# Four graph layers on one core: where layer 1's first four rows get their exponentials and logarithms, one scaling of layer 0's last rows, and which engine makes layer 1's bf16 casts

## The chip, the cores and the metric

The kernel runs on 1 core of one Trainium2 chip. The metric is the device time of one execution in microseconds (us), lower is better. The program is one launch; all four layers run in it one after the other.

## The reference, cut to what matters

The input is a field x of 8 batches, 2048 nodes and 64 features, and a symmetric 0/1 matrix adj of 2048 x 2048 with about eight neighbours a node. Four graph layers follow each other, each inside "add the input, then normalise over the 64 features". Layers 0 and 1 are the ones that matter here:

```
def _L0_gnn_ref(input, adj, W, a, ...):
    x = input * node_weights[None, :, None] + node_bias[None, :, None] + input
    h = layer_norm(x @ W) * ln_gamma + ln_beta
    e = leaky_relu(s1[:, :, None] + s2[:, None, :], 0.2)      # s1 = h.a1, s2 = h.a2
    att = softmax(where(adj > 0, e, -9e15), axis=-1)
    return elu(att @ h + h)

def _L1_gnn_ref(x, w0, b0, wa, ba, adj):
    feat = softplus(x * (INV_SQRT2 * w0[0, 0]) + b0[0])        # ln(1 + exp(.))
    scores = feat * wa + ba
    attn = softmax over the neighbours j of scores[j]           # per feature
    return sum_j attn * feat

x = _layernorm(x + _L0_gnn_ref(x, ...), axis=-1)
x = _layernorm(x + _L1_gnn_ref(x, ...), axis=-1)
...                                                             # layers 2 and 3
```

Since layer 1's score depends on the neighbour j alone, each node has one row of pairs (exp(score), exp(score) * feat), and layer 1 is a sum of these rows over the neighbours, followed by a division.

## The kernel before, in words

The 2048 nodes are 16 tiles of 128 (NT = 16; a tile is a partition dimension of 128 nodes, and 8 batches x 64 features = 512 values a node). X holds the field of all tiles and is updated in place.

Layer 0 first finds each node's neighbours from adj, and makes a table htab0 of h in memory. Then comes a pipeline of 17 steps, `step(0)` to `step(16)`. Step k handles tile k: GpSimd gathers its neighbours' rows (`fetch`, 10 indirect DMAs a tile, always one step ahead, three buffers hs), `weights` makes the attention weights (VectorE L598 and L601, ScalarE exponentials L602 and L603), `weigh` multiplies the gathered rows by them (VectorE L613, five a step) and TensorE adds them up (L621 values, L622 denominators). In the same step the tile before is finished: `divide(k-1)` (VectorE reciprocal L629, eight ScalarE scalings L632 of the sum po), `combine(k-1)` (VectorE L637, ScalarE exponential L639 into the tile e), `activate(k-1)` (VectorE L645, which reads e, and L648, which reads po for the last time), and `look_at(k-1)`, the statistics of the normalisation (L663). `solve` works out the inverse deviations for a group of tiles at a time (groups of 4, 4, 4, 2, 1 and 1), so a group of four is ready two steps after its last tile has been weighed. At the end of each step, `normalise` scales finished tiles on ScalarE (L183, eight instructions of 128x64 a tile); the last two tiles, 14 and 15, are scaled on VectorE after the steps (`normalise_here`, L683). Until the last tiles have been listed (step 12), the steps also carry the listing of neighbours of later tiles.

At the end of step 15 the kernel before makes feat for the first four tiles of layer 1: four exponentials (`exp_soon`, L699) and four logarithms (L764) into the tile `soon`, which lives through both layers.

Layer 1 makes its rows tile by tile. For tile t: `weight(t)` (VectorE L858: feat times wa; ScalarE L859: its exponential), `row(t)` (VectorE L863: the product with feat; SyncE L865: the row is written to the table rtab; and a cast of the row to bf16, on GpSimd L867 for odd t and on ScalarE L869 for even t), `second(t)` (VectorE L873: row minus its cast; ScalarE L874: that rest cast to bf16) and `third(t)` (VectorE L877: what is still left, as bf16). So a row is three bf16 pieces, and TensorE adds each piece into the sums of the first three output tiles (`add_piece`, L882, six matmuls of 512 columns a piece, 288 in all). feat for tiles 4 to 9 and 10 to 15 is made in two batches in between: exponentials one by one (`exp_of`, L847), and the logarithms of a batch together (`log_of`, L850). Then output tiles 3 to 7 are added from the pieces by dense products (`add_rows`, L817), mixed with tiles 8 to 15, whose neighbours' rows are gathered from rtab (`fetch` and `add_edges`, L946). The six sums of the first three output tiles take six of the eight PSUM banks; which banks these are is given by what layer 0 frees, and the last of layer 0 to be freed are those of tile 15: e after L645, po after L648.

The order of the work: steps 0 to 16 stand in one region in which the program's own order holds on TensorE, ScalarE, VectorE and GpSimd, and layer 1's row loop stands in a second such region. Within a region an engine's order is that of the program. The two regions are merged by the framework's scheduler: in the profile, instructions of the second region stand between those of the first on an engine (the eight L632 of tile 15, for instance, alternate with layer 1's L859, L847 and L869). [...] Layer 1's buffers lie in the memory that layer 0 has released: by the tile sizes in the code, the buffers of the row r lie over the gathered rows of tile 13, the first of them also over the end of tile 14's, and the pieces R of tiles 0 to 9 lie over what the listing used.

Of the kernel before, what the change touches and what calls it, by code (L numbers as in the profile page):

```python
# [48 lines left out]
def kernel(ctx: ExitStack, tc: tile.TileContext, ins: dict, out: bass.AP):  # L49
# [3 lines left out]
    NT = N // P  # L53
# [124 lines left out]
    def normed(chunks, stats):  # L178
        rstd, nmr = stats
        for c, v in enumerate(chunks):  # L180
            for b in range(B):
                k = c * B + b
                nc.scalar.activation(v[:, b], v[:, b], AF.Identity, scale=rstd[:, k:k + 1], bias=nmr[:, k:k + 1])  # L183
# [57 lines left out]
    SOON = 4  # L241
# [205 lines left out]
    def neighbours(it):  # L447
        on, plist, _, tops = lists[it]
        topf = tops.rearrange("p k m -> p (k m)")
        nbr = ap_.tile([P, SL + 1], F16, name="nbr")  # L450
        lists[it] = on, plist, nbr
        ops = []
        for k in range(0, SL, 8):
            ops.append(lambda k=k: nc.vector.max(nbr[:, k:k + 8], topf))
            if k + 8 < SL:
                ops.append(lambda k=k: nc.vector.match_replace(topf, nbr[:, k:k + 8], topf, 0.0))
        return ops

    def places(it):
        on, plist, nbr = lists[it]  # L460
        poff = plist[:, CW // 2 - 3:CW // 2]
        far_off = ap_.tile([P, 1], F32, name="far_off")
        nbrs = ap_.tile([P, NG, SL + 1], F16, name="nbrs")
        apart = ap_.tile([P, GE], F16, name="apart")
        lists[it] = on, plist, nbr, nbrs, apart

        def ended():
            nc.vector.scalar_tensor_tensor(ends[:, it:it + 1], offs[:, it:it + 1], -2.0, deg[:, it:it + 1], op0=ALU.mult, op1=ALU.subtract)
            nc.scalar.activation(apart, node_half, AF.Abs, scale=2.0, bias=ends[:, it:it + 1])

        return [lambda: nc.vector.tensor_reduce(far_off, poff, AX.X, ALU.max),
                lambda: nc.vector.tensor_scalar(offs[:, it:it + 1], far_off, 2.0 * GE, depth[:, 1:2], op0=ALU.min, op1=ALU.mult),
                ended,
                lambda: nc.vector.tensor_copy(nbr[:, SL:SL + 1], offs[:, it:it + 1]),
                lambda: nc.vector.tensor_tensor(nbrs, nbr.unsqueeze(1).to_broadcast(nbrs.shape),
                                                group.unsqueeze(2).to_broadcast(nbrs.shape), ALU.mult)]

    def tests(it):
        on, nbr = lists[it][0], lists[it][2]
        junk = ap_.tile([P, P], BF16, name="junk", bufs=1)  # L480
        return [lambda: nc.vector.scalar_tensor_tensor(junk, on[:, it * P:(it + 1) * P], 1.0, ident_bf, op0=ALU.mult, op1=ALU.mult,
                                                       accum_out=own_edge[:, it:it + 1]),
                lambda: nc.vector.scalar_tensor_tensor(junk[:, 0:SL], nbr[:, 0:SL], 0.0, nbr[:, 0:SL], op0=ALU.is_gt, op1=ALU.logical_and,
                                                       accum_out=listed[:, it:it + 1])]

    def select(it):
        _, plist, _, nbrs, apart = lists[it]
        nc.vector.tensor_scalar(SelT[:, it], apart, deg[:, it:it + 1], None, op0=ALU.is_lt, saturate=False)
        pl = plist[:, 1:1 + GS * NG * (SL + 1)].rearrange("p (g l) -> p g l", l=SL + 1)
        ps = plist[:, CW // 2:CW // 2 + GE].rearrange("p (s n) -> p s n", n=P)  # L490
        for s in range(GS):
            sel = SelT[:, it, s * P:(s + 1) * P]
            nc.tensor.matmul(pl[:, s * NG:(s + 1) * NG], sel, nbrs, start=True, stop=True)
            nc.tensor.matmul(ps[:, s], sel, ident_h, start=True, stop=True)
        lists[it] = pl, ps
# [63 lines left out]
    held, zs, stats = {}, {}, {}  # L559
# [117 lines left out]
    def normalise(it):  # L677
        normed([X[:, it]], stats.pop(it))

    def normalise_here(it):  # L680
        rstd, nmr = stats.pop(it)
        for b in range(B):
            nc.vector.tensor_scalar(X[:, it, b], X[:, it, b], rstd[:, b:b + 1], nmr[:, b:b + 1], op0=ALU.mult, op1=ALU.add)  # L683
# [5 lines left out]
    def interleaved(a, b):  # L689
# [5 lines left out]
                got.append(b.pop(0))  # L695
        return got

    def exp_soon(t):
        nc.scalar.activation(soon[:, t], X[:, t].rearrange("p b d -> p (b d)"), AF.Exp, scale=w0, bias=bb)  # L699

    def step(k):

        listed_, odd = AHEAD + k // 2, k % 2
        now, before_, ahead = k < NT, 1 <= k <= NT, k + 1 < NT
        early_, mid, late = [], [], []
        if odd and listed_ < NT:
            early_ = neighbours(listed_) + tests(listed_) + places(listed_)
            mid = [lambda: select(listed_)]
            if listed_ + 1 < NT:
                ats[listed_ + 1] = load(listed_ + 1)  # L710
        if not odd:
            if listed_ - 1 in lists:
                early_ = sources(listed_ - 1)
            if listed_ < NT:
                late = list_even(listed_)
        chain = []
        if k >= 2 and k - 2 < NT and k - 2 == norm_of[k - 2][-1]:
            chain = solve(norm_of[k - 2])
        if ahead:
            fetch(k + 1)  # L720
        main_a = weights(k) if now else []
        group = [weigh(k, n) for n in range(len(TOGETHER))] if now else [[]] * len(TOGETHER)
        if not odd and listed_ - 1 in lists:
            main_a.append(lambda: edges(listed_ - 1))
        main_a += group[0][:1]
        if before_:
            main_a.append(lambda: divide(k - 1))
        if ahead:
            main_a.append(lambda: prepare(k + 1))
        main_a += group[0][1:]  # L730
        main_b = group[1][:1]
        if before_:
            main_b.append(lambda: combine(k - 1))
        main_b += group[1][1:]
        main_b += activate(k - 1) if before_ else []
        main_c = list(group[2])
        main_c += look_at(k - 1) if before_ else []

        def run(main_, side, skip):
            done_, total = 0, len(side)  # L740
            for i, op in enumerate(main_):
                op()
                share = total * (i + 1 - skip) // max(1, len(main_) - skip)
                while done_ < share:
                    side[done_]()
                    done_ += 1
            for op in side[done_:]:
                op()

        half = (len(chain) + 1) // 2  # L750
        run(main_a, interleaved(early_[:len(early_) // 2], chain[:half]), 3)
        if ahead:
            scores(k + 1)
        if not odd and listed_ < NT:
            mark(listed_)
        run(main_b, interleaved(early_[len(early_) // 2:], chain[half:]), 0)
        for op in mid:
            op()
        run(main_c, late, 0)
        if k == NT - 1:  # L760
            for t in range(SOON):
                exp_soon(t)
            for t in range(SOON):
                nc.scalar.activation(soon[:, t], soon[:, t], AF.Ln, bias=ones_col)  # L764
        for t in sorted(stats)[:1 if k < NT - 3 else 2]:
            if t < NT - 2:
                normalise(t)

# [8 lines left out]
    with tc.manual_schedule(engines=engines):  # L777
        fetch(0)
        prepare(0)
        scores(0)  # L780
        for k in range(NT + 1):
            step(k)
        for op in solve(norm_of[NT - 2]) if norm_of[NT - 2] in sts else []:
            op()
        for op in solve(norm_of[NT - 1]):
            op()
        for t in sorted(stats):
            normalise_here(t)
    adj_.close()
    l0.close()  # L790

# [9 lines left out]
    with ExitStack() as l1:  # L801
# [50 lines left out]
        def split(v):  # L852
            return v.rearrange("p (h n) -> p h n", h=2)
# [7 lines left out]
        def row(t):  # L861
            r = rs_[t]
            nc.vector.tensor_tensor(r[:, :, 1], split(fs[t]), r[:, :, 0], ALU.mult)  # L863
            rf = r.rearrange("p h a n -> p (h a n)")
            nc.sync.dma_start(rtab[t * P:(t + 1) * P, :], rf)  # L865
            if t % 2:
                nc.gpsimd.tensor_copy(piece[t][0], rf)  # L867
            else:
                nc.scalar.copy(piece[t][0], rf)  # L869
# [460 lines left out]
    with early, ExitStack() as heads:  # L1330
# [261 lines left out]
        with tc.manual_schedule(engines=engines):  # L1592
# [37 lines left out]
            t = NT - 1  # L1630
# [17 lines left out]
    with ExitStack() as fifth:  # L1648
# [17 lines left out]
        hss, hsTs, pes, ws, wxs, zs, stats, sums = ({} for _ in range(8))  # L1666
# [257 lines left out]
    with tc.If(bad > 0), ExitStack() as anyway:  # L1924
# [88 lines left out]
        with ExitStack() as l0:  # L2013
# [71 lines left out]
            for b in range(B):  # L2085
                p, k = divmod(b, 2)
# [374 lines left out]
```

## Time and profile before

| | |
|---|---|
| Time, median of 3 runs | 1612.18 us (1601.11 to 1620.49) |
| The profiled execution's own time | 1768.37 us |
| Its span, first to last instruction | 1766.6 us |
| TensorE clock granted, mean over the span | 0.867 |
| TensorE busy | 1409.4 us (80%) |
| VectorE busy | 1165.4 us (66%) |
| ScalarE busy | 884.2 us (50%) |
| GpSimd busy | 790.0 us (45%) |

The profile is of one execution, and that one took 156 us longer than the median of the timed runs. Durations and waits are read from it as they stand; a difference that is worked out from it is a difference of the profiled execution. An engine's share of the span is an average over four layers with different limits; what counts for this change is the stretch from about 330 us (step 9 of layer 0) to about 670 us (the end of layer 1's products).

### The profile page before, as it was taken

The numbers are of one execution on the slowest core, as the hardware profiler recorded it, in microseconds if no ns is written. First come the engines' busy times: TensorE is split into PE (matmuls) and PEld (weight loads), VectorE is DVE, ScalarE is ACT, GpSimd is POOL, SyncE is SP. The second block draws the span as 40 slices with busy tenths as digits, with TensorE's granted clock in tenths as the row PEclk, the third lists the DMA queues.
The fourth block names the chain that finished last, engine by engine and source line by source line (L and its number), as shares of the span: only waits on it lengthen the run. The fifth ranks groups of instructions, "written<-read, shape, count | busy, mean of one in ns | idle before, by whom it ended". The sixth has DMA issues, their size and how long they took to land.

```text
span 1766.6 us, 39998 instructions
## 1 busy us (share of the span) xinstructions
PE 1409.4 (80%) x16140; PEld 956.7 (54%) x16140; DVE 1165.4 (66%) x2846; ACT 884.2 (50%) x1843; POOL 790.0 (45%) x786
## 2 busy tenths in 40 slices
PE   4775567755899996989728999998989679889884
PEld 4764233322343334522227777777777567777773
DVE  6787578776985646655834666666666536656667
ACT  4553245558833225445634565656555324555564
POOL 1234666661235552656433333343333156666651
PEclk9965575676899998999958999999999879888997
DMA  5434767662247971366434565656565365666651
GB/s 166 126 127 131 211 214 232 179 195 82 102 167 262 328 273 43 128 176 182 123 90 106 151 178 152 172 154 167 161 161 153 89 202 167 179 174 177 181 163 45
DMA packets 159322, 285.71 MB, mean 162 GB/s; under 512 B 68986, under 2 KB 94586, under 8 KB 157050
## 3 DMA queue, kind: packets, MB, share of 16 engines
q0 software_dynamic: 56320, 190.10, 36.5%
q1 hardware_dynamic: 86168, 88.78, 16.8%
q10 hardware_dynamic: 16640, 4.20, 1.0%
q8 instruction: 129, 2.11, 0.5%
q14 instruction: 65, 0.53, 0.1%
HBM read 242.52 MB, written 40.48 MB: 160 GB/s over the span
## 4 chain that ended last, share of the span: by engine, by line
PE 50%; DVE 9%; ACT 6%; issue 4%; DMA 1%; POOL 1%; another core or an unknown queue 1%; SPq 0%; POOLq 0%; ACTq 0%; DVEq 0%
PE pscore L1388 10%; PE po L1413 6%; PE pa L817 6%; PE ps L1716 4%; PE po L1755 4%; PE pt L1693 3%; PE pa L946 2%; PE pscore L1351 2%; PE pa L1290 2%; PE py L1120 2%; PE pscore L1480 2%; PE pe L1686 2%; PE pt L1000 2%; ACT w L1391 1%; DVE w_mid L1394 1%
## 5 line engine op out<-in xcount | busy, mean ns | idle before, releaser
L218 POOL DMA_INDIRECT xs<-xtab,src x160 | 171.8, 1074 | 280.8 <-PE po L1413 241.6
L218 POOL DMA_INDIRECT hs<-ktab,src x160 | 158.5, 991 | 140.2 <-DMA utab<-hT 47.7
L218 POOL DMA_INDIRECT hs<-htab,src x160 | 157.1, 982 | 88.5 <-issue 43.3
L1388 PE MATMUL pscore<-U,xsT 64*128 64x64 f32 (+2 forms) x2560 | 165.8, 280 | 1.1 <-ACT xsT L1375 1.1
L1388 PEld LDWEIGHTS pscore<-U,xsT 64*128 64x128 f32 x2560 | 155.2, 193 | 5.2 <-ACT xsT L1375 1.3
L1391 ACT ACTIVATE w<-pscore 128x512 f32<-128x512 f32 (+1 forms) x128 | 75.8, 622 | 139.7 <-PE pscore L1388 139.3
L1394 DVE SCALAR_TENSOR_TENSOR w<-w,Sel 128x512 f32<-128x512 f32 (+1 forms) x128 | 89.3, 722 | 79.2 <-ACT w L1391 61.1
L183 ACT ACTIVATE X<-X,ln_m,ln_r 128x64 f32<-128x64 f32 x240 | 81.4, 427 | 73.5 <-DVE ln_m L175 59.5
L1755 PE MATMUL po<-hs,w 128*32 128x65 f32 x2048 | 89.4, 236 | 32.3 <-issue 23.4
L1716 PE MATMUL ps<-U,hsT 128*128 128x64 f32 x768 | 104.5, 287 | 8.8 <-issue 5.8
L1716 PEld LDWEIGHTS ps<-U,hsT 128*128 128x128 f32 x768 | 103.0, 210 | 9.8 <-issue 6.0
L218 POOL DMA_INDIRECT rs<-rtab,src x80 | 75.9, 949 | 69.9 <-PE pa L946 47.5
L613 DVE TENSOR_TENSOR hs<-hs,w 128x1024 f32<-128x1024 f32 x80 | 96.7, 1213 | 11.1 <-ACT w L603 6.0
L817 PE MATMUL pa<-R,ET 128*128 128x512 bf16 x440 | 101.6, 380 | 0.0
L826 DVE RECIPROCAL rec<-pa 128x256 f32<-128x256 f32 x32 | 54.4, 1734 | 65.7 <-PE pa L946 41.6
L1755 PEld LDWEIGHTS po<-hs,w 128*32 128x32 f32 x2048 | 71.5, 119 | 45.1 <-issue 33.3
L1413 PE MATMUL po<-w,xs 128*64 128x64 f32 (+1 forms) x2048 | 84.4, 230 | 9.6 <-DVE o L1397 5.6
L218 POOL DMA_INDIRECT rs<-ytab,src x80 | 76.2, 953 | 35.0 <-issue 17.4
L1694 ACT COPY hsT<-pt 128x512 f32<-128x512 f32 x96 | 52.5, 586 | 77.8 <-remote 45.0
L1413 PEld LDWEIGHTS po<-w,xs 128*64 128x64 f32 x2048 | 71.4, 139 | 35.5 <-DVE w L1394 20.4
L1803 ACT ACTIVATE z<-z,ln_m,ln_r 128x64 f32<-128x64 f32 x240 | 83.4, 432 | 12.9 <-DVE ln_m L1791 12.9
L1290 PE MATMUL pa<-Y,ET 128*128 128x512 bf16 x384 | 89.4, 382 | 0.0
(673 smaller groups left out, 3355.3 us busy)
## 6 DMA issues: line engine op xcount, KB each, us to landing
at<-in_adj SPq DMA_DIRECT2D x16, 1024.0 KB
R<-itab SPq DMA_DIRECT2D x60, 256.0 KB
rtab<-r SPq DMA_DIRECT2D x16, 512.0 KB
ptab<-hp SPq DMA_DIRECT2D x16, 384.0 KB
hi<-ptab SPq DMA_DIRECT2D x16, 384.0 KB
htab<-H SPq DMA_DIRECT2D x16, 260.0 KB
own<-htab SPq DMA_DIRECT2D x16, 260.0 KB
ktab<-hb SPq DMA_DIRECT2D x16, 260.0 KB
```

Source lines behind the costliest of these rows:

```text
L183: nc.scalar.activation(v[:, b], v[:, b], AF.Identity, scale=rstd[:, k:k + 1], bias=nmr[:, k:k + 1])
L218: nc.gpsimd.indirect_dma_start(out=dst, out_offset=None, in_=table[:, :], in_offset=bass.IndirectOffsetOnAxis(ap=src[:, it, s, g:g + 1], a ...
L613: nc.vector.tensor_tensor(wx, wx, along(w[:, rows_]), ALU.mult)
L817: nc.tensor.matmul(po[h].rearrange("p a f -> p (a f)"), ET[:, jt, it * P:(it + 1) * P], piece[jt][q][:, h * BD:(h + 1) * BD], start=(jt == ...
L1290: nc.tensor.matmul(sums[it], ET[:, jt, it * P:(it + 1) * P], Y[:, jt, q].rearrange("p a n -> p (a n)"), start=(jt == 0 and q == 0), stop=( ...
L1388: nc.tensor.matmul(pscore[:, k_, f0:f0 + HN * ni].rearrange("p (h i) -> p h i", i=ni), xsT[half, p], Us[it][half, p, :, i0:i0 + ni], start ...
L1391: nc.scalar.activation(w.rearrange("p k a h i -> p k (a h i)"), pscore[:, :, 0:NP * HN * ni], AF.Exp)
L1394: nc.vector.scalar_tensor_tensor(wt, wt, 3.0e38, edge, op0=ALU.min, op1=ALU.mult)
L1413: nc.tensor.matmul(po[half, p, :, a - blk * GB:b - blk * GB], xs[:, f0:f0 + D], w[:, k_, p, :, a - WINDOWS[s][0]:b - WINDOWS[s][0]], start ...
L1716: nc.tensor.matmul(pscore[:, g, 2 * p:2 * p + 2], hsT[:, g, p], U[:, p, :, node_block(g, k)], start=False, stop=(p == NP - 1))
L1755: nc.tensor.matmul(po[node_block(g, k), j, b], w[:, g, t], hs[:, g, t], start=(s == BEGIN[k] and b == 0), stop=(s == END[k] and b == B // ...
L1803: nc.scalar.activation(v, v, AF.Identity, scale=r, bias=n)
```

## The change

Three edits. The exponentials of `exp_soon` no longer stand together at the end of step 15: step 9 has tile 0's, step 10 tile 1's, step 11 tile 2's, step 12 tile 3's, and all four logarithms stand at the end of step 12. The number of tiles that a step scales at its end is 2 in steps 13 and 14 and 1 elsewhere (before: 2 from step 13 on). So step 15 scales tile 12 alone, and tile 13's scaling comes at the end of step 16, behind the finishing of tile 15. And the cast of a row to bf16 is on GpSimd for tiles 3, 7, 11 and 15 (before: 1, 3, 5, 7, 9, 11, 13 and 15); the other twelve are on ScalarE.

```diff
+    SOON_FROM = 9
+
     def exp_soon(t):
         nc.scalar.activation(soon[:, t], X[:, t].rearrange("p b d -> p (b d)"), AF.Exp, scale=w0, bias=bb)
 ...
         run(main_c, late, 0)
-        if k == NT - 1:
-            for t in range(SOON):
-                exp_soon(t)
+        if 0 <= k - SOON_FROM < SOON:
+            exp_soon(k - SOON_FROM)
+        if k == SOON_FROM + SOON - 1:
             for t in range(SOON):
                 nc.scalar.activation(soon[:, t], soon[:, t], AF.Ln, bias=ones_col)
-        for t in sorted(stats)[:1 if k < NT - 3 else 2]:
+        for t in sorted(stats)[:2 if NT - 3 <= k < NT - 1 else 1]:
             if t < NT - 2:
                 normalise(t)
 ...
         for t in sorted(stats):
-            normalise_here(t)
+            if t < NT - 2:
+                normalise(t)
+            else:
+                normalise_here(t)
 ...
-            if t % 2:
+            if t % 4 == 3:
                 nc.gpsimd.tensor_copy(piece[t][0], rf)
             else:
                 nc.scalar.copy(piece[t][0], rf)
```

## The prediction

> **What bounds the kernel now.** I read the page's busy lines first: no engine fills the span, so a stretch has to be looked at by itself. The table of busy time by stretch cuts the passage from layer 0 to layer 1 in three: from the last matmul of step 15 to the start of layer 1's stream of products, the products that run while the rows are being made, and the rest of layer 1.
>
> ```profile
> core 0: us, PE busy (x) PEld busy (x) DVE busy (x) ACT busy (x) POOL busy (x), PEclk, DMA share, GB/s
> 428.20:449.40 21.20, 1.63 (x4) 0.27 (x4) 10.88 (x24) 21.15 (x45) 1.04 (x1) 0.53 0.18 74
> 449.40:518.50 69.10, 66.00 (x286) 28.78 (x287) 59.70 (x91) 45.12 (x59) 23.88 (x13) 0.95 0.32 123
> 518.50:669.00 150.50, 150.50 (x864) 55.27 (x862) 88.68 (x216) 36.54 (x104) 71.11 (x86) 1.00 0.77 272
> ```
>
> The first stretch has TensorE busy 1.63 of 21.2 us and ScalarE 21.15 of 21.2: ScalarE is the bound there. From 449.4 on TensorE is the bound (66.0 of 69.1, then 150.5 of 150.5). So a microsecond by which TensorE's stream starts earlier is one at the end, as long as the rows keep up. ScalarE's timeline shows what fills the gap:
>
> ```profile
> 423.69 2.92 ACT L699 ACTIVATE soon<-X,bb,w 128x512 f32<-128x512 f32 x4
> 426.63 1.28 ACT L764 ACT_TABLE_LOAD   x1
> 427.92 2.56 ACT L764 ACTIVATE soon<-soon,ones_col 128x512 f32<-128x512 f32 x4
> 430.39 5.40 ACT L183 ACTIVATE X<-X,ln_m,ln_r 128x64 f32<-128x64 f32 x16
> 435.69 0.26 ACT L632 ACTIVATE po<-po,rd 128x64 f32<-128x64 f32 x1
> 435.97 1.28 ACT L859 ACT_TABLE_LOAD   x1
> ...
> 443.08 0.30 ACT L632 ACTIVATE po<-po,rd 128x64 f32<-128x64 f32 x1
> ```
>
> The exponentials, the table, the logarithms and two tiles' scalings run to 435.7; only then come the eight L632 of tile 15, spread over 435.69 to 443.38 because layer 1's instructions stand between them. VectorE and TensorE at the same time:
>
> ```profile
> 429.29 0.20 DVE L629 RECIPROCAL rd<-pe 128x8 f32<-128x8 f32 x1
> ...
> 437.92 0.69 DVE L863 TENSOR_TENSOR r<-soon,r 128x512 f32<-128x512 f32 x1 [7.12 <-ACT r L859]
> ...
> 448.54 0.68 DVE L648 SCALAR_TENSOR_TENSOR X<-po,X 128x512 f32<-128x512 f32 x1
> ```
>
> ```profile
> 427.93 0.25 PE L622 MATMUL pe<-wm,self__3353 128*32 128x8 f32 x8
> 442.51 0.58 PE L882 MATMUL pa<-R,ET 128*128 128x512 bf16 x1 [14.34 <-ACT R L869]
> 447.39 1.01 PE L882 MATMUL pa<-R,ET 128*128 128x512 bf16 x2 [4.29 <-DVE X L645]
> 449.37 8.05 PE L882 MATMUL pa<-R,ET 128*128 128x512 bf16 x27 [0.97 <-ACT R L874]
> ...
> 477.09 25.16 PE L882 MATMUL pa<-R,ET 128*128 128x512 bf16 x108 [2.06 <-POOL R L867]
> ```
>
> The reciprocal is ready at 429.5, six microseconds before ScalarE takes it up. L645 ends at 447.33 and two products start at 447.39; L648 ends at 449.22 and the stream starts at 449.37, whatever releaser is named. These are the two PSUM banks of tile 15. So the bound is the chain reciprocal, L632, L637, L639, L645, L648 of tile 15, and ScalarE is what makes it late.
>
> **What the Trainium skill says.** "ScalarE: Activation LUTs", section "What ACT_TABLE_LOAD costs", prices a switch of table at about 1283 ns plus a drain of about 1380 ns; the trace has the 1.28 us and nothing of the drain (426.63 to 427.92). The section "Table sets: the hidden batching unit" counts one load for ln and then exp; this trace has a second one at 435.97 on the way back, so I count two for a visit to the logarithm. "SBUF — State Buffer", section "SBUF: two separate sides", says that GpSimd and VectorE lock each other out of a shared pair of ports for a whole instruction; the trace agrees in kind: the cast L867 takes 1.04 to 4.32 us for one shape, and L877 beside it 2.05 instead of 1.21. "Perfetto Trace Analysis", section "Tensor Engine Instruction (MATMUL, LD_WEIGHTS)", says that TensorE's ends are estimates; I use that at step 13 below.
>
> **Part 1, taken from step 15.** Four exponentials 2.92, a table 1.28, four logarithms 2.56: 6.8 us off ScalarE's path. Tile 13's scaling, half of 5.40, moves behind tile 15's L639: 2.7. The exponential table is in place when layer 1's first L859 comes: 1.28. Together 10.8 us less ahead of L648. Only part of that is gain, since ScalarE then waits for the reciprocal at 429.5, 6.2 us before 435.69.
>
> What is late next: the new start is the last matmul of step 15 (428.18), plus 0.8 from part 2, plus two layer-1 instructions of 0.6 on VectorE that now fall into step 15, 430.2. The reciprocal ends 1.3 later as before (429.49 minus 428.18): 431.5. The eight L632 took 2.54 us alone (419.49) and 7.7 mixed with layer 1's work and a table; much of that work will be done by then in ScalarE's idle time of step 15, so I take 4.8: 436.3. L637, L639, L645 and L648 are 0.7 + 0.6 + 0.7 + 0.7 and about 0.9 of handing over: 439.9. TensorE's stream starts at about 440 instead of 449.4: 9.4 us. Bounds: all 7.7 kept and the rest as long as before (5.8) gives 445, a gain of 4.4; nothing mixed in, 431.5 + 2.5 + 3.6 = 437.6, less the 1.2 of VectorE, is 436.4, a gain of 13.0.
>
> **Do the rows keep up?** VectorE needs 0.6 + 0.6 + 1.14 + 1.13 = 3.5 us a row (spacing of its timeline), TensorE 18 products of 0.2155 = 3.9. VectorE's waits of 0.89, 7.12, 0.33 and 2.26 between 428 and 442 were all for ScalarE; as `soon` is ready at step 12, rows 0 to 2 can begin once the buffer r is free, after step 14's last matmul at about 417.7 (the last 768 bytes of tile 14's rows lie under the first r). So VectorE moves ahead by about as much as TensorE.
>
> **Part 2, added to steps 9 to 12.** Steps 9, 10 and 11 get 0.73 us each (2.92 / 4), ahead of the scaling; ScalarE then sits idle for 3.3 to 5.1 us until the next L602. They cost nothing; without that cover, 0.73 each. Step 12 gets 0.73 + 1.28 + 2.56 and 1.28 for the way back: 5.85 us, against 1.93 idle:
>
> ```profile
> 384.00 2.75 ACT L183 ACTIVATE X<-X,ln_m,ln_r 128x64 f32<-128x64 f32 x8
> 388.68 0.24 ACT L602 ACTIVATE wm<-w 128x80 f32<-128x80 f32 x1 [1.93 <-DVE wm L598]
> ```
>
> ```profile
> 389.07 1.22 DVE L613 TENSOR_TENSOR hs<-hs,w 128x1024 f32<-128x1024 f32 x1 [0.43 <-issue]
> 393.55 0.21 DVE L629 RECIPROCAL rd<-pe 128x8 f32<-128x8 f32 x1 [3.25 <-remote]
> ```
>
> So L602 of step 13 is 3.9 us late. Behind it on ScalarE stand L603 and tile 12's L632; VectorE's first L613 waits for it, 389.07 becoming 393.0, ending 394.2. But L629 of this step waits until 393.55 anyway: GpSimd's next gather, at 393.74, is let go at the same moment, so step 12's matmuls ended near 393.4 and not at their estimated 388.6. That hides all but 0.7 to 0.8. Bounds: 0 and 3.9; I take 0.8. No DMA is issued by what is moved. The exponentials pass no wait; the logarithms wait for nothing that is not on their own engine.
>
> **Part 3, the casts.** Four casts go from GpSimd (1.04 to 4.32) to ScalarE at 1.04 each, 4.2 us over 80 us in which ScalarE has idle time (45.1 busy of 69.1). TensorE's waits for GpSimd were 2.06 (row 5) and 0.58 (row 13); both rows are on ScalarE now. Rows 3, 7, 11 and 15 can still clash with L877, so I take 2.0 of the 2.6 as gain; bounds: minus 1 (ScalarE's casts late behind a batch of logarithms) and plus 3.5.
>
> **The sum.** 9.4 (the 0.8 of step 13 is in it) + 2.0 = 11.4 us: the span 1766.6 becomes 1755.2, and the execution's 1768.4 becomes 1757.0. What is saved is waiting on ScalarE and VectorE[...], so I take the same microseconds from the median: 1612.2 - 11.4, about 1601.
>
> **The rivals.**
> Rows set the pace: VectorE, not TensorE, bounds the rows. For it: the chain that ended last runs through VectorE's L873, L877, L858 and GpSimd's cast up to 502.8. Against it: 3.5 against 3.9 us a row. Then the earlier start buys only a few of the removed waits: gain about 4, 1608 us.
> All of it pays: L632 unmixed, every GpSimd wait gone, 13.0 + 3.5 = 16.5: 1596 us. Against it: L632 was mixed before.
> Slower: layer 1's early rows are placed in ScalarE's and VectorE's queues ahead of step 15's own instructions. A row held there costs the round L858, L859, L863, cast, 0.69 + 0.63 + 0.69 + 1.04 = 3.1 us, and L602, L613 and tile 15's matmuls stand behind it. Two such instructions are in my sum; from 11.4 us, about 3.7 whole rows, it decides, and with all four rows of `soon` and step 13's full 3.9 instead of 0.8 the sum is 11.4 - 12.4 - 3.1, 4 us slower: 1616. For it: the scheduler merges the two regions already; against it: it does so where an engine would wait.
>
> **How the numbers follow.** Forecast 0.52, rows set the pace 0.20, all of it 0.14, slower 0.14. The cases lie within 1596 to 1616, and medians of few runs add to it (three runs here span 1601 to 1620): 1585 to 1617. About 1%, 16 us, is what a measurement of this kernel can tell from no change, so most of the forecast falls within it: faster by over 1% 0.28 (a quarter of the forecast, over half of "all of it" and some chance besides), within 1% 0.65, slower 0.07.
>
> **What would show it.** Right: no L699 or L764 after step 12; two tables around step 12; L602 of step 13 near 392.6 with step 13's L629 hardly later; L632 of tile 15 starting within 2 us of its reciprocal; TensorE's stream starting near 440 and L882 ending near 507; no table ahead of the first L859. "TensorE: Matmul & The Clock Gate", section "What's actually happening", has an idle TensorE throttled; the granted 0.53 from 428 to 449 agrees, and a shorter gap should lift it. Wrong: a stream that starts before 445 with L882 still ending near 518 (the rows), or step 15's last matmul later than 433 (the slower case).

## The result, and the profile after

| | before | after |
|---|---|---|
| Median of 22 runs each, us | 1607.51 (1600.52 to 1620.49) | 1600.82 (1594.29 to 1609.20) |
| after / before, 95% interval | | 0.9959 (0.9939 to 0.9978) |
| The profiled execution: time, span, us | 1610.83, 1608.9 | 1608.76, 1606.5 |

The kernel became 6.7 us faster (3.5 to 9.8 by the interval), where 11.4 were forecast; that gain lies outside the interval, though the change stays within 1%, the likeliest case of the prediction. That the forecast of about 1601 lies so near to 1600.8 is luck: its base, a median of three runs, was 4.7 us above that of the 22, its gain was 4.7 too large, and the two cancel. The profile on which the prediction rested was of an execution 156 us longer than the median of those three runs; the kernel before was therefore profiled once more (`e0_before`), and that profile is the "before" of everything below.

The stretch from layer 0 to layer 1 was divided at five events, in each kernel: the exponential L602 of step 8, the end of step 15's last matmul, the moment when the last two PSUM banks are free and the products run in a stream, the end of the products for the first three output tiles (the stream while rows are made), and the end of layer 1's products.

| us | before (e0) | after | difference |
|---|---|---|---|
| L602 of step 8 to the last matmul of step 15 | 101.10 | 105.66 | +4.56 |
| from there to the stream | 21.19 | 12.94 | -8.25 |
| the stream while rows are made | 69.15 | 68.42 | -0.73 |
| from there to the end of layer 1's products | 151.05 | 151.33 | +0.28 |
| sum | 342.49 | 338.35 | -4.14 |

So the change pays 8.25 us at the end of step 15 and takes back 4.56 before it. The busy times of the stretches, first before, then after (stretch, its length, then busy us of TensorE, weight loads, VectorE, ScalarE and GpSimd, the granted TensorE clock, the DMA share, GB/s; the first line of each is step 12, from L602 to L602):

```profile
341.48:352.08 10.60, 8.31 (x50) 4.10 (x54) 10.13 (x22) 7.44 (x24) 7.92 (x9) 0.68 0.67 201
387.20:408.40 21.20, 1.18 (x3) 0.27 (x4) 10.84 (x24) 21.15 (x45) 1.04 (x1) 0.55 0.18 74
408.40:477.50 69.10, 65.92 (x281) 28.95 (x287) 59.71 (x91) 45.15 (x59) 23.85 (x13) 0.94 0.32 123
```

```profile
342.60:357.15 14.55, 7.47 (x70) 3.71 (x62) 10.16 (x22) 13.24 (x31) 10.69 (x12) 0.83 0.72 213
392.30:405.20 12.90, 1.61 (x4) 0.25 (x3) 10.77 (x28) 12.90 (x33) 0.00 (x0) 0.54 0.30 122
405.20:473.60 68.40, 64.39 (x286) 28.60 (x287) 57.19 (x86) 50.88 (x64) 19.91 (x11) 0.96 0.33 128
```

Step 12 grows from 10.60 to 14.55, and ScalarE's busy time in it by 5.8, which is the moved work. The gap shrinks, but ScalarE is still busy for all of its 12.90 us: it stays the bound there, now with layer 1's own work.

In ScalarE's timeline of the kernel after, step 12's end has the batch with its two table loads, and the next L602 follows at once:

```profile
348.51 0.80 ACT L701 ACTIVATE soon<-X,bb,w 128x512 f32<-128x512 f32 x1
349.34 1.28 ACT L766 ACT_TABLE_LOAD   x1
350.63 2.56 ACT L766 ACTIVATE soon<-soon,ones_col 128x512 f32<-128x512 f32 x4
353.09 2.75 ACT L183 ACTIVATE X<-X,ln_m,ln_r 128x64 f32<-128x64 f32 x8
355.86 1.28 ACT L602 ACT_TABLE_LOAD   x1
357.15 0.24 ACT L602 ACTIVATE wm<-w 128x80 f32<-128x80 f32 x1
```

The kernel before had ScalarE idle for 1.93 us at this place. VectorE's side, before (first fence) and after (second):

```profile
352.48 1.22 DVE L613 TENSOR_TENSOR hs<-hs,w 128x1024 f32<-128x1024 f32 x1 [0.43 <-ACT w L603]
353.61 0.20 DVE L629 RECIPROCAL rd<-pe 128x8 f32<-128x8 f32 x1
```

```profile
357.55 1.22 DVE L613 TENSOR_TENSOR hs<-hs,w 128x1024 f32<-128x1024 f32 x1 [4.39 <-ACT w L603]
358.69 0.20 DVE L629 RECIPROCAL rd<-pe 128x8 f32<-128x8 f32 x1
```

In both, the reciprocal L629 follows the first L613 directly. The wait of 3.25 us that was to hide the late L602 is in neither of these two profiles.

At the end of step 15, ScalarE after:

```profile
390.03 2.77 ACT L183 ACTIVATE X<-X,ln_m,ln_r 128x64 f32<-128x64 f32 x8 [2.12 <-DVE ln_m L674]
393.03 0.62 ACT L864 ACTIVATE r<-r 128x512 f32<-128x512 f32 x1
393.55 0.26 ACT L632 ACTIVATE po<-po,rd 128x64 f32<-128x64 f32 x1
...
399.73 0.29 ACT L632 ACTIVATE po<-po,rd 128x64 f32<-128x64 f32 x1
...
401.81 0.61 ACT L639 ACTIVATE e<-po 128x512 f32<-128x512 f32 x1
402.32 2.77 ACT L183 ACTIVATE X<-X,ln_m,ln_r 128x64 f32<-128x64 f32 x8
```

VectorE and TensorE at the same time:

```profile
391.84 0.67 DVE L863 TENSOR_TENSOR r<-soon,wa 128x512 f32<-128x512 f32 x1
392.43 0.21 DVE L629 RECIPROCAL rd<-pe 128x8 f32<-128x8 f32 x1
...
404.42 0.69 DVE L648 SCALAR_TENSOR_TENSOR X<-po,X 128x512 f32<-128x512 f32 x1
```

```profile
403.27 1.01 PE L887 MATMUL pa<-R,ET 128*128 128x512 bf16 x2 [4.41 <-DVE X L645]
405.25 8.46 PE L887 MATMUL pa<-R,ET 128*128 128x512 bf16 x27 [0.97 <-DVE ln_r L144]
...
416.78 2.75 PE L887 MATMUL pa<-R,ET 128*128 128x512 bf16 x12 [1.78 <-POOL R L872]
...
442.43 31.24 PE L887 MATMUL pa<-R,ET 128*128 128x512 bf16 x144 [2.19 <-ACT R L874]
```

The reader sees the chain of tile 15 intact: reciprocal at 392.43, L632 from 393.55 to 400.02, L639 at 401.81, L648 ending at 405.11, the stream at 405.25, whatever releaser is named. No table stands ahead of the first L864. The exponential L701 and the logarithms L766 are gone from here, and tile 13's L183 comes behind L639. In the stream, two waits are left, 1.78 for a GpSimd cast (tile 3) and 2.19 for a ScalarE cast (tile 9); before there were 0.26 for ScalarE, and 2.06 and 0.59 for GpSimd's casts of tiles 7 and 13.

### The profile page after: what moved, and what is told of

Read it like the earlier page. It is cut to its first block, busy times and chain, and to the rows that moved or that the text cites. A ratio compares the mean times of both kernels' runs of the same rounds, so it can differ in the third digit from the quotient of the medians.

```text
span 1606.5 us, 39997 instructions
## 1 busy us (share of the span) xinstructions
PE 1329.6 (83%) x16140; PEld 922.8 (57%) x16140; DVE 1162.9 (72%) x2846; ACT 894.3 (56%) x1847; POOL 781.8 (49%) x782
## 4 chain that ended last, share of the span: by engine, by line
PE 52%; DVE 18%; ACT 11%; issue 5%; POOL 5%; DMA 3%; SPq 0%; DVEq 0%; ACTq 0%; POOLq 0%
PE pscore L1393 10%; PE po L1418 6%; PE pa L822 6%; PE pscore L1356 4%; POOL hs L218 4%; PE pt L1005 3%; PE pa L951 3%; PE ps L1721 3%; PE pa L1295 2%; ACT X L183 2%; PE po L1760 2%; PE pa L887 2%; DVE hs L613 2%; PE py L1125 2%; PE pscore L1485 2%
## 5 line engine op out<-in xcount | busy, mean ns | idle before, releaser
L218 POOL DMA_INDIRECT xs<-xtab,src x160 | 167.9, 1049 | 241.2 <-PE po L1418 211.5
L1396 ACT ACTIVATE w<-pscore 128x512 f32<-128x512 f32 (+1 forms) x128 | 79.7, 623 | 92.8 <-PE pscore L1393 88.4
L183 ACT ACTIVATE X<-X,ln_m,ln_r 128x64 f32<-128x64 f32 x240 | 81.5, 428 | 76.6 <-DVE ln_m L175 72.2
L613 DVE TENSOR_TENSOR hs<-hs,w 128x1024 f32<-128x1024 f32 x80 | 96.8, 1215 | 15.6 <-ACT w L603 15.6
L1721 PE MATMUL ps<-U,hsT 128*128 128x64 f32 x768 | 95.5, 271 | 1.1 <-ACT hsT L1699 1.1
L1721 PEld LDWEIGHTS ps<-U,hsT 128*128 128x128 f32 x768 | 94.2, 195 | 1.4 <-ACT hsT L1699 1.3
L1808 ACT ACTIVATE z<-z,ln_m,ln_r 128x64 f32<-128x64 f32 x240 | 83.4, 430 | 12.9 <-DVE ln_m L1796 12.9
L1380 ACT COPY xsT<-pt 128x1024 f32<-128x1024 f32 x80 | 80.9, 1011 | 10.9 <-PE pt L1005 10.9
L822 PEld LDWEIGHTS <-ET 128*128 128x128 fp8e4 x480 | 45.0, 98 | 71.1 <-issue 19.3
L1760 PE MATMUL po<-hs,w 128*32 128x65 f32 x2048 | 72.9, 225 | 6.8 <-DVE w L1733 6.8
```

The lines of the kernel that those rows point to most:

```text
L218: nc.gpsimd.indirect_dma_start(out=dst, out_offset=None, in_=table[:, :], in_offset=bass.IndirectOffsetOnAxis(ap=src[:, it, s, g:g + 1], a ...
L613: nc.vector.tensor_tensor(wx, wx, along(w[:, rows_]), ALU.mult)
L822: nc.tensor.matmul(po[h].rearrange("p a f -> p (a f)"), ET[:, jt, it * P:(it + 1) * P], piece[jt][q][:, h * BD:(h + 1) * BD], start=(jt == ...
L1380: nc.scalar.copy(unflipped(xsT), pt.rearrange("p k s a n -> p k (s a) n"))
L1721: nc.tensor.matmul(pscore[:, g, 2 * p:2 * p + 2], hsT[:, g, p], U[:, p, :, node_block(g, k)], start=False, stop=(p == NP - 1))
L1760: nc.tensor.matmul(po[node_block(g, k), j, b], w[:, g, t], hs[:, g, t], start=(s == BEGIN[k] and b == 0), stop=(s == END[k] and b == B // ...
```

## The experiments

Each expectation names its theories by letters. A: the batch in step 12 makes step 13 late by its full price, 3.9 us. B: it is hidden but for 0.8. C: a microsecond by which the stream starts earlier is one at the end of layer 1. D: the rows set the pace, and a good part of an earlier start turns into waits for rows. E stands for a rival that the one expectation naming it spells out. "Trace" below is the change of the sum of the first table against e0, from one profiled execution each. Such a sum is uncertain by a microsecond or two: the part behind the stream, which is the same in both, took 150.69 us in e3 and 151.33 in the kernel after, and a stretch of slower TensorE clock, which comes and goes (last section), can add 1.7.

**The kernel before again (e0).** No edit.

> The kernel before, unchanged, for a second profile of it: the one that the prediction was read from took 156 us more than the median of the timed runs, and the profile of the changed kernel did not. Theory A (the logarithms in step 12 cost their full 3.9 us in step 13, since the 3.25 us for which step 13's reciprocal L629 waited in the first profile are not there in an ordinary execution): L629 of step 13 follows L613 at once, and step 13's L613 waits about 0.5 us for ScalarE. Theory B (the cost in step 13 is hidden as forecast, 0.8 us): a wait of about 3 us ahead of L629 of step 13 is there again. Both: about 21 us from step 15's last matmul to the stream of L882, time within 0.5% of the kernel before.

Its ScalarE, the L602 of steps 10, 11, 12 and 13, with the idle time ahead of each in brackets:

```profile
314.09 0.24 ACT L602 ACTIVATE wm<-w 128x80 f32<-128x80 f32 x1 [0.20 <-DVE w L601]
329.63 0.24 ACT L602 ACTIVATE wm<-w 128x80 f32<-128x80 f32 x1 [5.03 <-DVE w L601]
341.48 0.24 ACT L602 ACTIVATE wm<-w 128x80 f32<-128x80 f32 x1 [0.32 <-DVE w L601]
352.08 0.24 ACT L602 ACTIVATE wm<-w 128x80 f32<-128x80 f32 x1 [1.93 <-DVE w L601]
```

The room at the end of a step is 5.03 us only after steps 8 and 10; after 9 and 11 it is 0.20 and 0.32. In the kernel after, the intervals from L602 to L602 grew by 0.29 (step 9), 0.30 (step 11) and 3.95 (step 12): 4.54 of the 4.56 us. A is right, B is not. VectorE's "remote" waits in the first profile of before are absent here:

```profile
DVE wm L598 <- remote: 10.0, 3, 3.5
```

That line is from the first profile (VectorE, 315 to 390 us): 10.0 us in 3 waits, each about as long as the wait that the prediction relied on. "Remote" means that the profile doesn't show what ended them; L598 reads the gathered rows, so late gathers are a likely reading, but not a shown one.

**The move of the exponentials and logarithms alone (e1).**

```diff
+    SOON_FROM = 9
 ...
-        if k == NT - 1:
-            for t in range(SOON):
-                exp_soon(t)
+        if 0 <= k - SOON_FROM < SOON:
+            exp_soon(k - SOON_FROM)
+        if k == SOON_FROM + SOON - 1:
             for t in range(SOON):
```

> Only the exponentials and logarithms are moved to steps 9 to 12; tile 13 is still scaled in step 15 and the odd casts stay on GpSimd. Theory A: the stream of products starts about 5.6 us earlier after step 15's last matmul (8.3 us as in the changed kernel, less 2.7 of tile 13's scaling that stands before L632 again), step 13 gives back 3.3: about 2 us faster than before, ratio 0.9985. Theory B: step 13 gives back 0.8: about 5 us faster, ratio 0.997.

Ratio 0.9990 (0.9974 to 1.0007). Trace: steps +4.52, gap 15.33 instead of 21.19, sum -1.55. By itself the move gains 5.86 us in the gap and gives 4.52 of it back. The kernel after has a gap of 12.94, and the casts alone leave it at 21.19 (e2), so the moved scaling of tile 13 is worth 2.4.

**The casts alone (e2).**

```diff
-            if t % 2:
+            if t % 4 == 3:
```

> Only the casts: GpSimd makes those of tiles 3, 7, 11 and 15, ScalarE the rest. Theory A: TensorE's waits for GpSimd are exchanged for waits for ScalarE behind the second batch of logarithms; within 1 us of the kernel before, ratio 0.9993 to 1.0007. Theory B (the forecast's 2.0 us): ratio 0.9988, and TensorE's waits in L882 add up to under 1.5 us.

Ratio 1.0003 (0.9979 to 1.0026); trace -0.21. TensorE's waits in the stream became 1.00, 0.26 and 2.39 for ScalarE and 1.65 for GpSimd, in place of 2.06 and 0.59 for GpSimd and 0.26 for ScalarE. One wait for GpSimd is left, that for tile 7, whose cast stays there, and tile 9's cast made a new one of 2.39 on ScalarE: the waits grew by 2.4 us in all, and no gain is left. That there is no loss either goes with TensorE's clock: in the four microseconds behind the wait for tile 7 it was 1.00 here and 0.62 in e0.

**The same change two steps earlier (e3).** The exponentials in steps 7 to 10 and the logarithms in step 10, where ScalarE has 5.03 us of room.

```diff
-    SOON_FROM = 9
+    SOON_FROM = 7
```

> The changed kernel with everything of soon two steps earlier: exponentials in steps 7 to 10, logarithms in step 10, after which ScalarE sat idle for 5.1 us in the first profile. Theory A: the 3.9 us of step 13 fall away and at most 1 us comes up in step 11; 2.5 to 3.5 us faster than the changed kernel, ratio to the kernel before about 0.994. Theory B: no difference from the changed kernel, ratio about 0.996.

Ratio 0.9939 (0.9917 to 0.9960). Trace: -8.26 against -4.14 of the kernel after; the gap (12.92) and the stream are the same, and the steps cost 1.10 instead of 4.56 (the remaining 0.6 lie behind the stream, where the two kernels don't differ). ScalarE at the end of step 10 does what it did at the end of step 12, but the table load now ends just after the next exponential could have begun:

```profile
322.83 1.28 ACT L766 ACT_TABLE_LOAD   x1
324.12 2.56 ACT L766 ACTIVATE soon<-soon,ones_col 128x512 f32<-128x512 f32 x4
326.59 2.74 ACT L183 ACTIVATE X<-X,ln_m,ln_r 128x64 f32<-128x64 f32 x8
329.35 1.28 ACT L602 ACT_TABLE_LOAD   x1
330.65 0.24 ACT L602 ACTIVATE wm<-w 128x80 f32<-128x80 f32 x1
```

This interval grew by 0.84, which is the moved 5.85 (0.73 + 1.28 + 2.56 + 1.28) less the 5.03 of idle time. The price of step 12's batch is thus its excess over that step's idle time, and nothing else. In timed runs the intervals of e3 and of the kernel after overlap; that e3 is the faster one rests on the trace.

**Tile 15's division by one VectorE instruction, on top of e3 (e5).** The eight L632 of tile 15 are those that ScalarE mixes with layer 1's work.

```diff
-        for b in range(B):
-            nc.scalar.activation(z[:, b], z[:, b], AF.Copy, scale=rd[:, b:b + 1])
+        if it == NT - 1:
+            nc.vector.tensor_tensor(z, z, along(rd), ALU.mult)
+        else:
+            for b in range(B):
+                nc.scalar.activation(z[:, b], z[:, b], AF.Copy, scale=rd[:, b:b + 1])
```

> The kernel with the logarithms in step 10, and tile 15's eight ScalarE scalings L632 replaced by one VectorE product of 128x512. Theory C (the stream of L882 starts when tile 15 has left its PSUM banks, and what is still late there is L632 mixed with layer 1's instructions, 6.5 us instead of 2.5; each microsecond at the start is one at the end): in this kernel's order six of layer 1's instructions still stand ahead of the exponential e, about 4.7 us, so the stream starts about 9.0 us after step 15's last matmul instead of 12.9, the products take 68.4 us as before, and the time is about 4 us below that with the logarithms in step 10: ratio to the kernel before about 0.9915. Theory D (the rows set the pace): the gap shrinks to 9 us as well, but the products take about 72 us and the ratio stays at 0.994.

Ratio 0.9938 (0.9914 to 0.9962); trace -9.37. The banks came free 8.17 us after step 15's last matmul instead of 12.92, but layer 1 ended only 1.15 earlier than in e3. TensorE:

```profile
397.01 1.46 PE L890 MATMUL pa<-R,ET 128*128 128x512 bf16 x3 [0.35 <-DVE X L651]
399.12 7.36 PE L890 MATMUL pa<-R,ET 128*128 128x512 bf16 x24 [0.65 <-ACT R L877]
...
411.21 1.46 PE L890 MATMUL pa<-R,ET 128*128 128x512 bf16 x6 [2.36 <-POOL R L875]
```

Against e3's two waits in the stream (1.78 and 2.19) these are 0.65, 2.36 and 2.37, 1.41 us more. The rest went in TensorE's clock: behind the wait of 2.37 the same products took longer than in e6, the next run. Here is that stretch of e5, then of e6:

```profile
437.27:470.20 32.93, 32.93 (x145) 14.63 (x145) 24.56 (x25) 14.91 (x17) 13.27 (x10) 0.95 0.46 171
```

```profile
435.94:467.18 31.24, 31.24 (x145) 14.16 (x145) 24.56 (x25) 14.90 (x17) 12.05 (x9) 1.00 0.44 163
```

1.69 us at a clock of 0.95 instead of 1.00, all of it in the first four microseconds (0.57 there). So of the 4.75 us that the banks gained, 1.4 turned into waits for rows, 1.7 into a slower clock and the rest, but for half a microsecond, arrived. VectorE's timeline says why. Its product for tile 9's row, in e3 and in e5:

```profile
433.01 0.68 DVE L868 TENSOR_TENSOR r<-R,r 128x512 f32<-128x512 f32 x1
```

```profile
431.92 0.68 DVE L871 TENSOR_TENSOR r<-R,r 128x512 f32<-128x512 f32 x1
```

That is 44.75 and 43.08 us after step 15's last matmul. The banks came free 4.75 us earlier, the row only 1.67, and the wait for tile 9's cast, the stream's last, ended 1.67 earlier too (438.36 in e3, 437.27 here). C fails from here on, D holds. (With this edit some of the dense products of layer 1, L825, stand inside the stream, so only whole sums are compared.)

**Tile 3's cast on ScalarE too (e6).** On top of e5.

```diff
-            if t % 4 == 3:
+            if t % 4 == 3 and t > 3:
```

> The kernel before this one with tile 3's cast moved from GpSimd to ScalarE as well (GpSimd keeps 7, 11 and 15). Theory C: TensorE's wait of about 1.8 us for GpSimd's cast of tile 3 goes, and a wait for ScalarE behind its first batch of logarithms comes instead; within 1 us of the kernel before this one. Theory D: the products get up to 2 us shorter.

Ratio 0.9917 (0.9892 to 0.9943); trace -11.94, of which layer 1 has 2.62 more than e5. The wait for GpSimd is gone; what replaced it:

```profile
410.71 2.75 PE L890 MATMUL pa<-R,ET 128*128 128x512 bf16 x12 [2.27 <-ACT R L877]
...
435.94 31.24 PE L890 MATMUL pa<-R,ET 128*128 128x512 bf16 x144 [1.76 <-ACT R L877]
```

TensorE's idle time in layer 1 is 12.0 us in e5 and in e6. All of the 2.6 is busy time of TensorE (218.92 against 216.26), and most of that is the clock just shown. So by its waits this edit gains nothing that the trace shows; whether it avoids the slow clock or e6 met none by chance is open.

**The division edit alone, on the kernel before (e7).** The edit of e5.

> The kernel before with one edit: tile 15's eight L632 replaced by one VectorE product; soon, scalings and casts as before. e follows tile 13's scaling and a table on ScalarE, so both theories put the banks free about 11 us after step 15's last matmul; the first cast of row 0 then comes at about 13.4 us, which is the start of the stream (21.2 before). Theory C: the products take no more than 70 us: about 7 us faster, ratio 0.9955. Theory D: the rows have no lead now, the products take 73 us or more and the gain is 4 us or less, ratio 0.9975.

Ratio 0.9961 (0.9941 to 0.9981); trace -4.92. (The recorded end of step 15's last matmul is 0.9 later in this profile, while L602 and the reciprocal of that step stand as in e0, so the sum is used.) The first product and the row that cost most:

```profile
399.43 9.49 PE L885 MATMUL pa<-R,ET 128*128 128x512 bf16 x30 [12.78 <-ACT R L872]
...
415.42 2.70 PE L885 MATMUL pa<-R,ET 128*128 128x512 bf16 x6 [3.69 <-POOL R L870]
```

L648's counterpart ended at 397.36, so the banks were free 2.07 us before TensorE had its first row: without the move of the exponentials the first row is what is late, and GpSimd's cast of tile 3, 4.25 us from 411.11 on, holds TensorE for another 3.69. The products took 73.2 us, as D has it, while the time is near C's ratio. This one edit thus measures as much as the whole change, in time and in the trace.

**Row before logarithms (e8).** On top of e6: where a batch of logarithms follows, the row n-1 and its first piece are issued ahead of it, not behind.

```diff
+                    row(n - 1)
+                    add_piece(n - 1, 0)
 ...
-                if 1 <= n <= NT:
+                if 1 <= n <= NT and n not in STARTS:
```

> The kernel with tile 3's cast on ScalarE and the division of tile 15 on VectorE, and in addition the row (product, cast and first piece) of tiles 3 and 9 placed ahead of the batch of logarithms instead of behind it. Theory D (the rows set the pace, through the casts that stand behind the logarithms on ScalarE; TensorE waited 2.27 and 1.76 us for them): both waits shrink, layer 1's products end about 2 us earlier, ratio to the kernel before about 0.990. Theory E (it only changes places: the logarithms and with them weight(4) and weight(10) come later by what the casts take): the waits move to tiles 4 and 10, no gain, 0.9917.

Ratio 0.9899 (0.9868 to 0.9930); trace -11.00, not better than e6's -11.94. The waits moved again:

```profile
414.22 1.95 PE L890 MATMUL pa<-R,ET 128*128 128x512 bf16 x5 [2.86 <-ACT R L882]
...
440.15 29.95 PE L890 MATMUL pa<-R,ET 128*128 128x512 bf16 x136 [0.77 <-ACT R L882]
```

The wait ahead of the last long run fell from 1.76 to 0.77, the one ahead of it rose from 2.27 to 2.86, and the last run began 42.44 us after the first product in the last bank (397.71) instead of 40.80. What is late now are the second pieces of tiles 2 and 8, whose casts (L882) still stand behind the logarithms. It has the lowest ratio measured, but the intervals of e5, e6, e8 and e10 overlap, and the trace doesn't support an order.

**Tile 3's cast on ScalarE, division as it was (e9).** On top of e3, the edit of e6.

> The kernel with the logarithms in step 10, tile 3's cast moved to ScalarE, and tile 15's L632 left as eight ScalarE instructions. Theory D: TensorE's wait for GpSimd of 1.78 us goes and the end of layer 1's products comes about 1 us earlier; without the faster division the rest of the 2.6 us that the same edit gave with it is not there: ratio about 0.993. Theory E: all 2.6 us come from the cast itself, ratio about 0.9923.

Ratio 0.9946 (0.9926 to 0.9966); trace -7.50, no gain on e3's -8.26.

```profile
417.20 2.75 PE L887 MATMUL pa<-R,ET 128*128 128x512 bf16 x12 [3.09 <-ACT R L874]
```

Where ScalarE still has tile 15's scalings, the 1.78 for GpSimd becomes 3.09 for ScalarE. The row was ready at 412.52 here, but on ScalarE its cast stands behind the first batch of logarithms and ran from 416.12 to 417.15. In the kernel after the row was ready at 412.95, GpSimd began at 413.09 and took 3.63. So the place in ScalarE's queue makes the cast late on the one engine, its length on the other.

**Two casts on GpSimd, tiles 9 and 15 (e10).** On top of e6; it aims at the wait for tile 9.

```diff
-            if t % 4 == 3 and t > 3:
+            if t in (9, 15):
```

> As the kernel with tile 3's cast on ScalarE and the division on VectorE, but GpSimd makes the casts of tiles 9 and 15 (instead of 7, 11 and 15): tile 9's is the one that stood behind the second batch of logarithms (TensorE's wait of 1.76 us). Theory D: that wait goes, unless the cast meets VectorE's L885 and takes over 2 us, in which case a wait for GpSimd of about the same length comes in its place; ratio 0.9905 to 0.992.

Ratio 0.9940 (0.9922 to 0.9958); trace -13.22, the best of all.

```profile
436.76 8.58 PE L890 MATMUL pa<-R,ET 128*128 128x512 bf16 x39 [0.57 <-ACT R L882]
```

The wait at this place fell from 1.76 to 0.57 (it is now for the second piece of tile 8), and layer 1 ended 1.19 earlier than in e6: the wait and the end agree. The time doesn't confirm it: its interval overlaps e6's, but lies above the 0.9905 to 0.992 that were expected. A microsecond is below what these runs tell apart.

## Why the prediction was right, and where it was wrong

The side was right, and so was the cause of the gap: ScalarE's late start on tile 15's L632 kept the stream waiting, and its relief starts the stream earlier (5.86 us by the exponentials and logarithms alone, e1). The rival "rows set the pace" forecast a gain of about 4, and the trace has 4.14, but not by its mechanism: the stream took no longer for its earlier start (68.42 against 69.15 us, and 69.2 in e1, where the casts are as before), while 4.56 us went into the steps. Its mechanism shows beyond this change (e5). The sizes were off in all three parts. Of the prediction's signs of being right, the two tables around step 12, the late L602 of step 13, the early L632 and the missing table ahead of L864 came true. Two did not: step 13's L629 came 4.5 us late with its L602, and the stream's last product came 4.4 us earlier, counted from step 8's L602, where 11.5 were forecast.

**Part 1, the stream's start: 11.4 us forecast from step 15's last matmul (21.2 to 9.8), 8.25 measured.** (These 11.4 are the prediction's 9.4 before it took off 0.8 for step 13 and 1.2 for VectorE; that they equal its total is chance.) Term by term, with the forecast first:

| us | forecast | measured |
|---|---|---|
| last matmul to the end of the reciprocal | 1.3 | 0.33 |
| ScalarE takes it up after | 0 | 0.91 |
| the eight L632 | 4.8 | 6.47 |
| L637, L639, L645, L648 and handing over | 3.7 | 5.23 |
| sum | 9.8 | 12.94 |

The first term was too long because the kernel before had a layer-1 L858 ahead of the reciprocal that waited 0.89 us for the logarithms; with these done earlier that wait went. The second was left out: tile 12's scaling started 2.12 us late, for ln_m, and was followed from 392.70 on by three small setup instructions and an L864. The third and fourth terms are the mis-sized ones. "Much of that work will be done by then in ScalarE's idle time of step 15" was wrong: the first L863 stands at 391.84, directly before the reciprocal, as its counterpart did before, so no more row work than before was pulled into step 15, and all of it is still mixed in with L632 and with what follows (L639 waited behind two casts, L648 behind an L882 of 1.22). For the same reason the 1.2 us that VectorE was to lose in step 15 didn't occur, and the case "slower", whose mechanism is just that pull, got no support. That case's other ingredient, the full 3.9 us in step 13, did come true: step 15's last matmul came 4.56 us later, just short of the 4.8 that stood for this case. The bounds that the prediction gave for the stream's start (436.4 and 445, so 7.4 and 14.8 us after the last matmul) hold the 12.94; the value taken between them was too good.

**Part 2, steps 9 to 12: 0.8 forecast, 4.54 measured.** The step that failed is "L629 of this step waits until 393.55 anyway". That wait was real in the profile, but it was one of the "remote" waits of one long execution; e0 has none, and the upper bound of 3.9 (measured 3.95) was the answer. "They cost nothing" of steps 9 to 11 failed in the same way: the idle time of 3.3 to 5.1 us that was read after each of them is 5.03 after step 10 only. e3 confirms the cause: the same work with 5.03 us of room costs 0.84.

**Part 3, the casts: 2.0 forecast, 0.73 measured in the stream, and nothing when made alone (e2).** The prediction read TensorE's wait of 2.06 us as one for row 5. It is row 7's: GpSimd casts the odd tiles in order, and its fourth cast ends just ahead of the product at 436.11 (e0):

```profile
431.74 4.31 POOL L867 CAST R<-r 128x1024 bf16<-128x1024 f32 x1 [10.40 <-DVE r L863]
```

Row 7 stays on GpSimd in this change, so of the 2.6 us that were to be gained only row 13's 0.59 lay within the edit's reach. In e2 the wait for row 7 is there, 1.65; in the kernel after, the cast is as long (4.31 from 427.76 on), but TensorE, held before it by 1.78 us at tile 3, finds it done. What was late next is ScalarE's cast of tile 9 behind the second batch of logarithms, at 2.19; the prediction named this case but put it into its lower bound only. GpSimd's cast of tile 3 (3.63 us) makes the other wait:

```profile
413.09 3.63 POOL L872 CAST R<-r 128x1024 bf16<-128x1024 f32 x1 [45.28 <-ACT R L855]
```

**One to one to the end.** The gap's 8.25 us and the stream's 0.73 arrive at layer 1's end less 0.28, so in sum an earlier start did pay in full. But that TensorE is the bound from there on was not right: the stream's last wait is for a row, tile 13's in e0 and tile 9's in the kernel after, and this row decides when the stream ends. The rows came forward with the start. VectorE's product for tile 9's row, in e0 and in the kernel after:

```profile
441.07 0.69 DVE L863 TENSOR_TENSOR r<-R,r 128x512 f32<-128x512 f32 x1
```

```profile
437.08 0.69 DVE L868 TENSOR_TENSOR r<-R,r 128x512 f32<-128x512 f32 x1
```

That is 53.86 and 44.77 us after step 15's last matmul, 9.09 earlier. Relief of ScalarE helps the banks and the rows alike, since both come out of its queue; this change doesn't separate the two, e5 does. Less 4.56 that leaves 4.14 by the trace and 6.7 (3.5 to 9.8) by the timed runs. The rest of the span, behind layer 1, is untouched, but took between 971.9 (e3) and 985.9 us (e1) in these profiles, which is why one pair of profiles can't be summed to the span.

**TensorE's clock.** "A shorter gap should lift it" was wrong: 0.54 was granted over the gap of 12.9 us and 0.55 over that of 21.2.

What stays open: whether e6, e8 or e10 is the best version. Each beats both kernels, the kernel before by its ratio and the kernel after by the trace (-11.0 to -13.2 against -4.1); e8 has the lowest ratio, e10 the best trace. Taken beside the same runs of the kernel before, e8's median is 1592.3 us (6 runs) and e10's 1598.0 (16 runs), while e10's trace is 2.2 us better. Also open is what the first profiled execution waited for in its "remote" waits.

## What to carry to other kernels

Work moved into another engine's slack costs its length less the idle time at that very place, so read the idle time step by step (here it alternated between 0.2 and 5 us), and move it to the step that has the most. Don't let a single wait hide a cost before a second profile shows that wait too, above all when the profiled execution is longer than the timed ones. Count the products ahead of a wait before you say which row it is for. And once the start of a stream is early enough, look at the two or three producers it waits for next: taking a cast from one engine mostly moved the wait to the other.

## What the runs showed of the hardware that was not expected

- A wait of TensorE can cost more than its length. Behind waits of 2.06 us (e0), 2.37 (e5), 2.86 (e8) and 3.69 (e7) the granted clock fell for some four microseconds, to 0.57 in e5 and e7; behind waits of 2.06 (e1), 2.19 (after), 2.27 (e6), 2.39 (e2) and 3.09 (e9) it stayed at 1.00. In e0, e7 and e8 a later wait for a row follows, which can take the loss up: e1, with the same wait as e0 and no slow stretch, then waited 1.09 and 1.03 us where e0 waited 0.59, and in both the stream ended 41.4 us after the wait. In e5 no later wait follows, and there the 1.69 us show at the end. "TensorE: Matmul & The Clock Gate", section "What's actually happening", has the throttle come back after at least one idle window of about 3.4 us that runs free of the program; that the same wait does or doesn't trigger it fits such a window, but 2.06 us was enough here.
- The way to the logarithm and back took two table loads of 1.28 us each, and the next instruction began 0.01 us after each (349.34 to 350.63, 355.86 to 357.15).
- In the one execution that was 156 us longer than the median of its three runs, VectorE had three waits, 10.0 us in all, that the profile names only "remote", at places where e0 had none.
